# A slot per expert, three more by row number, and a folded bias in wide products (perceiver block, one core of a Trainium2 chip)

## The chip, the core and the metric

The kernel runs on one core of one Trainium2 chip. A core has a matrix engine (PE, with its own loader of stationary operands, PEld), a vector engine (DVE), an activation engine (ACT), a general engine (POOL) and a queue that only issues transfers (SP). POOL issues transfers too, those whose rows are picked by an index in memory ("indirect"). All transfers run on the core's 16 DMA engines. Each engine takes its own instructions in program order, and waits for others by semaphores. The metric is the time of one execution on the device in microseconds, as the median of several runs.

## What is computed

Two layers of a perceiver: x is 8 x 64 = 512 rows of 512 numbers, the context 8 x 1601 rows. The part that matters here is the end of layer 0 and the start of layer 1:

```python
x = x + _L0_xattn_ref(_layernorm(x), ctx_1024, ctx_1024, ...)
x = x + _L0_attn_ref(_layernorm(x), ...)          # a gated scan
x = x + _L0_ffn_ref(_layernorm(x), ...)           # eight experts, one per row
x = x + _L1_xattn_ref(ctx_1024, ctx_1024, _layernorm(x), Wk, Wv, bv, Wq, bq, Wo, bo)

def _L0_ffn_ref(x, router_w, router_b, expert_w, expert_b):
    probs = softmax(x @ router_w + router_b)
    gate, idx = max(probs), argmax(probs)
    e_out = x @ expert_w[idx] + expert_b[idx]     # expert_w: 8 x 512 x 512
    return gate * e_out

# in _L1_xattn_ref: scores = (q Wq^T + bq)(k Wk^T)^T / sqrt(512)
```

All arithmetic is in float32. An expert's weights are 1 MB. In layer 1 the kernel multiplies Wq and Wk into one matrix ahead of time ("folds" them), and then bq with Wk into one vector of 512 (`wqk_b`); Wv and Wo are folded as well.

## The kernel before

**Experts by slots.** A router gives each of the 512 rows one of eight experts. The rows are scattered to a scratch array in memory (`xsd`) so that rows of one expert lie together in blocks of 128, called slots. `SLOTS = 11` slots are enough for any routing: each expert's rows take as many slots as they need, one after the other. `places()` (L924) counts rows per expert on PE, works out on DVE where each row goes (`posi`, L950) and which expert each of the 11 slots belongs to (`wrow`, row numbers into the table of weights, L960 to L968), and has POOL scatter the rows (L953).

`slots()` (L1089) then runs over the 11 slots. `fetch(s)` (L1095) loads the 1 MB of the slot's expert into one of `WE = 4` tiles `we`, by an indirect transfer on POOL with row numbers from `wrow`. `rows(s)` (L1101) loads the slot's 128 rows (256 KB) on SP. `turn(s)` (L1105) transposes them on PE, ACT copies them out, and four products on PE (L1123) give the slot's result, which DVE copies out and SP stores to `ysd` (L1126). In turn s of the loop the order is: products of s, store of s, `fetch(s + 4)`, `rows(s + 4)`, `turn(s + 2)`. Fetches of slots 1 to 3 stand behind a POOL copy (`seen`, L1113) in the code. After the last slot POOL gathers the results back by `posi` (L1139), and x is updated (L1141).

**The work between routing and slots.** `fold_qk()` (L983) multiplies Wq and Wk: it transposes Wq into the tile `wqT`, multiplies with the tile `wk1`, and last computes `wqk_b` by 16 products whose moving operand is one column of bq (L988 to L992). `wk1` and `wqT` are tiles of the pool that held the keys of layer 0. After that pool is closed, new pools take over its memory: `wp` (weight and context tiles `w`), `md`, and `we`. `expert_bias()` (L1165) multiplies the expert biases (tile `eb`, 8 x 512) with the gates; `fold_vo()` (L1152) transposes Wv and multiplies it with Wo; the second half of that product runs after the slots.

**What sets the order.** PE's order is written out by `interleave` (L244): threads yield estimated durations, and the thread with the lowest rank that is due goes next. The order is then fixed: PE runs it as written, waiting where an operand isn't there. SP's order is the program's order too from L1576 on (`manual_schedule` of SP, until L1145). There stand, in this order: `eb` (16 KB), `cst` (448 KB), Wv and Wo (1 MB each, in halves), eight context tiles (512 KB each, for the scores of layer 1), a bias row, and then what `slots()` issues. A transfer also waits, on SP, until the eighth transfer before it has landed.

Of the kernel before, what the change touches and what calls it, by code (L numbers as in the profile page):

```python
# [16 lines left out]
NT = 4  # L17
DC = 4
SK = 1601
E, FF, CAP = 8, 2048, 64  # L20
WE = 4
SLOTS = 11
CH = [(0, 512), (512, 512), (1024, 512), (1536, 65)]
KC = [(0, 384), (384, 384), (768, 384), (1152, 449)]
SB = [(i * 128, min(128, SK - i * 128)) for i in range(13)]
# [19 lines left out]
def perceiver_kernel(ctx: ExitStack, tc: tile.TileContext, a: dict, out: bass.AP):  # L45
# [304 lines left out]
    ohs, wgt = [sm([128, NT, E], nm, 1) for nm in ("ohs", "wgt0")]  # L350
    gates = sm([128, NT], "gates", 1)
    posi = small.tile([128, NT], mybir.dt.int32, tag="posi", name="posi", bufs=1)
    wrow = small.tile([128, SLOTS], mybir.dt.int32, tag="wrow", name="wrow", bufs=1)
    xsd, ysd = [tc.dram_tile((SLOTS * 128, D), F32, name=nm) for nm in ("xsd", "ysd")]


    with ExitStack() as st:
# [20 lines left out]
        def bank(*shape):  # L378

            return ps("bk", shape or (128, 512), 7)  # L380
# [393 lines left out]
        for b in range(B):  # L774
            if b == 1:

                zero = sm([128, 64], "zero", 1)
                nc.gpsimd.memset(zero, 0.0)
                for s in range(SLOTS):
                    nc.sync.dma_start(  # L780
                        xsd[ts(s, 128), :].rearrange("p (r c) -> p r c", c=64), zero.unsqueeze(1).to_broadcast([128, 8, 64])
                    )
            if b == B - 1:

                for i in (2, 1, 0, 3):
# [12 lines left out]
                tri0, ones0, iota0 = [c3[:, ts(i, 128)] for i in range(3)]  # L798
                nc.vector.tensor_mul(c3[:, 384:], iota0, ident)
                line = sm([128, 1], "sl_line", 1)  # L800
                nc.vector.reduce_sum(line, c3[:, 384:], axis=AX.X)
                steps = sm([128, NT], "sl_steps", 1)
                nc.vector.tensor_scalar_mul(steps, iota0[:, :NT], 128.0)
                rw0 = sm([128, DC, E], "rw0", 1)
                nc.sync.dma_start(rw0, a["L0_ffn_router_w"].rearrange("(p c) e -> p c e", c=DC))
                rb0 = sm([128, E], "rb0", 1)
                nc.sync.dma_start(rb0, a["L0_ffn_router_b"].partition_broadcast(128))
            if b % 2 == 0:
                oU = xq.tile([128, DC, 128], F32, tag="oX", name=name("oU"), bufs=2)
                rq = sm([128, 16], "rq")  # L810
            if b == B - 1:
                break
            queries(b + 1)
            if b % 2:
                load_tail((b + 1) // 2)
            load_unit(b + 1, 0)
            fill = products(b + 1)

            def project(n):
                for _ in range(n):  # L820
                    next(ahead, None)
                    next(fill)

            pa = ps("pa", (128, DC, 128))


            for ec, (na, nb, nc_, nd) in enumerate(((2, 3, 2, 3), (2, 3, 2, 3), (1, 3, 2, 3), (2, 3, 3, 5))):
                att = attend(b, ec, *got.pop(ec), pa, rq)
# [24 lines left out]
            run(fill)  # L853
# [70 lines left out]
        def places():  # L924
# [7 lines left out]
            for t in range(NT):  # L932
                mm(total, ones0, ohs[:, t, :], t == 0, t == NT - 1)
            work = xq.tile([128, D], F32, tag="oX", name="work", bufs=2)
            full = work[:, : E * NT].rearrange("p (e k) -> p e k", e=E)
            nc.vector.tensor_tensor(
                full, total.unsqueeze(2).to_broadcast([128, E, NT]), steps.unsqueeze(1).to_broadcast([128, E, NT]), ALU.is_gt
            )
            used, upto = work[:, 32:40], work[:, 40:48]
            nc.vector.reduce_sum(used, full, axis=AX.X)  # L940
            nc.vector.tensor_tensor_scan(upto, ones0[:, :E], used, 0.0, ALU.mult, ALU.add)
            nc.vector.tensor_sub(used, upto, used)
            place = work[:, 64:96].rearrange("p (t e) -> p t e", e=E)
            nc.vector.scalar_tensor_tensor(
                place, used.unsqueeze(1).to_broadcast([128, NT, E]), 128.0, rank, ALU.mult, ALU.add
            )
            nc.vector.tensor_mul(place, place, ohs)
            pos = work[:, 96 : 96 + NT]
            nc.vector.reduce_sum(pos, place, axis=AX.X)
# [2 lines left out]
            for t in range(NT):  # L952
# [4 lines left out]
                    tc.declare_no_dep(i.ins, other.ins, reason="no two tokens have the same place")  # L957
                scatters.append(i)

            past = work[:, 128 : 128 + SLOTS * E].rearrange("p (s e) -> p s e", e=E)  # L960
            nc.vector.tensor_tensor(
                past, upto.unsqueeze(1).to_broadcast([128, SLOTS, E]),
                iota0[:, :SLOTS].unsqueeze(2).to_broadcast([128, SLOTS, E]), ALU.is_le,
            )
            whose = work[:, 256 : 256 + SLOTS]
            nc.vector.reduce_sum(whose, past, axis=AX.X)
            nc.vector.tensor_scalar(whose, whose, float(E - 1), 128.0, ALU.min, ALU.mult)
            nc.vector.tensor_scalar(wrow, whose, line, None, ALU.add)  # L968
# [14 lines left out]
        def fold_qk():  # L983
            yield ready[3]
            w_k, turned_ = key_tile("wk1", a["L1_xattn_Wk"]), key_tile("wqT")
            yield 5000.0
            yield from fold([w_q[:, c, :] for c in range(DC)], [w_k[:, c, :] for c in range(DC)], wqk, turned_, bank)
            p = bank()  # L988
            for e in range(DC):
                for d in range(DC):  # L990
                    mm(p[:, e : e + 1], w_k[:, d, ts(e, 128)], col("L1_xattn_bq", d), d == 0, d == 3)
            nc.vector.tensor_copy(wqk_b, p[:, :DC])  # L992

        for t in range(NT - 1):
            scan_norm(t, free[t][:, 0, :])
# [93 lines left out]
    def slots():  # L1089


        table = a["L0_ffn_expert_w"].rearrange("e (p c) d -> (e p) (c d)", c=DC)
        ws, xs, xsT = {}, {}, {}

        def fetch(s):  # L1095
            ws[s] = we.tile([128, DC * D], F32, tag="we", name=name("we"))
            nc.gpsimd.indirect_dma_start(
                ws[s], None, table, bass.IndirectOffsetOnAxis(ap=wrow[:, s : s + 1], axis=0)
            )

        def rows(s):  # L1101
            xs[s] = t2("xs")
# [6 lines left out]
        fetch(0)  # L1109
        for s in range(4):  # L1110
            rows(s)

        nc.gpsimd.tensor_copy(seen, xs[1][:, 0:1])  # L1113
        for s in range(1, WE):
            fetch(s)
        yield 13000.0
        for s in range(2):
            turn(s)
# [1 line left out]
        for s in range(SLOTS):  # L1120
            p = ps("pp")
            for c in range(DC):
                mm(p, xsT[s][:, ts(c, 128)], ws[s][:, ts(c, D)], c == 0, c == 3)  # L1123
            y = t2("ys")
            nc.vector.tensor_copy(y, p)
            nc.sync.dma_start(ysd[ts(s, 128), :], y)  # L1126
            if s + WE < SLOTS:
                fetch(s + WE)
            if s + 4 < SLOTS:
                rows(s + 4)  # L1130
            if s + 2 < SLOTS:
                turn(s + 2)
            if s == 7:

                sooner[0, 2] = context(0, 2)
            yield 0.0
# [434 lines left out]
        mh["o"], mh["wo"] = oT, wo  # L1571

    biased, asked, folded = [Event() for _ in range(3)]
    seen = md.tile([128, 1], F32, tag="seen", name="seen", bufs=1)
    in_order = ExitStack()
    in_order.enter_context(tc.manual_schedule(engines={mybir.EngineType.SP}))  # L1576
    nc.sync.dma_start(eb, a["L0_ffn_expert_b"])
    nc.sync.dma_start(cst, a["cst"])
    for n in "vo":
# [222 lines left out]
```

## Time and profile before

| What | us |
|---|---|
| median of 3 runs | 1608.79 (1601.51 to 1611.84) |
| the profiled execution, whole | 1610.92 |
| its span, first to last instruction | 1609.1 |
| PE busy in it | 1543.5 |
| from the products of `wqk_b` to the first slot's transposes | 1044.55 to 1067.71 |
| the eleven slots on PE | 1067.71 to 1119.1 |
| PE idle while the results are gathered and normalized | 5.62 and 2.14, before 1135.06 and 1138.28 |

The span is 1.8 us short of the profiled execution's time, and that execution is 2.1 us above the median. In the views, times count from the span's start. A row of the timeline gives the start, the duration, the engine (SPq and POOLq are the issuing of transfers), the source line, output and input tiles, and in brackets how long the engine had been idle before and what released it. A row of the stages gives the stretch, its length, the busy time of each engine with its instructions, the granted clock of PE as a share of full speed, the busy share of the DMA engines, and what they moved in GB/s.

### The profile page before, as it was taken

What the parts mean: (1) busy time and instruction counts of PE and PEld (TensorE: products, weight loads), DVE (VectorE), ACT (ScalarE), POOL (GpSimd) and SP (SyncE); (2) the same over time, 40 slices, a digit from 0 to 9 for tenths busy, and PEclk for the clock granted to TensorE, in tenths of its full rate; (3) what the DMA queues carried; (4) which work ended last, traced back from release to release, by engine and by line L of the source; (5) the groups of instructions that cost most, each with busy time, mean ns of one, the idle gap of its engine ahead of it and who ended that gap; (6) DMA issues with size and microseconds to landing.
All of it is one profiled execution on the core that took longest, in us unless ns stands there. A gap on an engine that the chain in (4) does not pass through costs nothing. (4 is left out here: it accounts for less than half of the span.)

```text
span 1609.1 us, 23036 instructions
## 1 busy us (share of the span) xinstructions
PE 1543.5 (96%) x9452; PEld 1123.9 (70%) x9452; DVE 719.8 (45%) x1678; ACT 291.0 (18%) x495; POOL 228.3 (14%) x274
## 2 busy tenths in 40 slices
PE   8999999999999999999999999999899898989996
PEld 6778888888888878888888868954444456654432
DVE  5245555445545455554555666521322344341213
ACT  1111212212122212122221231111001111200000
POOL 5211111111110111211021000111200121120000
PEclk9999999999999999999999999989999999979999
DMA  8100110010111111010111320478799650619995
GB/s 254 44 27 27 34 27 27 27 53 27 34 27 27 40 40 34 27 35 20 46 34 31 97 75 1 177 253 289 274 371 362 242 210 1 229 47 374 378 387 205
DMA packets 129193, 197.64 MB, mean 123 GB/s; under 512 B 27825, under 2 KB 53169, under 8 KB 127681
## 3 DMA queue, kind: packets, MB, share of 16 engines
q1 hardware_dynamic: 126864, 182.54, 33.8%
q0 software_dynamic: 2224, 13.63, 2.3%
q8 instruction: 75, 1.23, 0.3%
q14 instruction: 30, 0.24, 0.0%
HBM read 188.28 MB, written 7.86 MB: 122 GB/s over the span
## 5 line engine op out<-in xcount | busy, mean ns | idle before, releaser
L466 PE MATMUL bk<-pc,Tk 128*128 128x256 f32 x768 | 179.4, 382 | 0.2 <-POOL pc L403 0.2
L510 PE MATMUL bk<-Tv,pc 128*128 128x256 f32 x768 | 179.4, 382 | 0.0
L593 DVE TENSOR_SCALAR_CACHE_REDUCE s<-bk 128x512 f32<-128x512 f32 (+1 forms) x256 | 131.9, 572 | 101.2 <-PE bk L230 100.9
L466 PEld LDWEIGHTS bk<-pc,Tk 128*128 128x128 f32 x768 | 142.5, 190 | 29.3 <-issue 5.3
L510 PEld LDWEIGHTS bk<-Tv,pc 128*128 128x128 f32 x768 | 142.9, 190 | 23.9 <-issue 5.3
L466 PE MATMUL bk<-pc,k 128*128 128x256 f32 x576 | 136.7, 386 | 6.1 <-DMA pc<-in_ctxT_dram 6.1
L605 ACT ACTIVATE s<-s,sx_nm 128x1601 f32<-128x1601 f32 x64 | 103.9, 1626 | 193.0 <-DVE sx_nm L602 177.9
L510 PE MATMUL bk<-v,pc 128*128 128x256 f32 x576 | 134.2, 380 | 0.0
L493 DVE TENSOR_TENSOR kT<-bk,tm 128x512 f32<-128x512 f32 x96 | 66.4, 692 | 131.1 <-PE bk L466 130.4
L466 PEld LDWEIGHTS bk<-pc,k 128*128 128x128 f32 x576 | 109.5, 193 | 22.2 <-issue 7.8
L402 POOL TENSOR_TENSOR pc<-pc,pc 128x512 f32<-128x512 f32 x24 | 30.5, 1272 | 655.6 <-PE bk L510 285.4
L510 PEld LDWEIGHTS bk<-v,pc 128*128 128x128 f32 x576 | 108.1, 190 | 15.8 <-issue 1.4
L629 ACT COPY pT<-bk 128x512 f32<-128x512 f32 x96 | 56.3, 586 | 292.3 <-PE bk L235 290.9
L235 PE MATMUL bk<-ident,s 128*128 128x128 f32 (+1 forms) x832 | 103.4, 274 | 0.0
L230 PE MATMUL pa<-pT,vU 128*64 128x128 f32 x1536 | 99.3, 277 | 3.6 <-ACT pT L629 3.6
L230 PE MATMUL bk<-kT,qbd 64*128 64x512 f32 x384 | 102.7, 642 | 0.0
L235 PEld LDWEIGHTS bk<-ident,s 128*128 128x128 f32 (+1 forms) x832 | 93.1, 141 | 12.4 <-issue 5.2
L230 PEld LDWEIGHTS pa<-pT,vU 128*64 128x64 f32 x1536 | 82.4, 137 | 26.4 <-issue 18.9
L526 DVE TENSOR_TENSOR vU<-bk,tm 128x512 f32<-128x512 f32 x96 | 66.4, 692 | 72.1 <-PE bk L510 71.1
L631 DVE COPY pT<-bk 128x512 f32<-128x512 f32 (+1 forms) x128 | 75.5, 616 | 14.5 <-PE bk L235 13.9
L94 POOL TENSOR_SCALAR ln_rs<-ln_mv 128x1 f32<-128x1 f32 x32 | 10.8, 338 | 404.3 <-DVE ln_mv L1604 188.5
L230 PE MATMUL pa<-w,hT 128*64 128x512 f32 x256 | 58.6, 597 | 1.1 <-DMA w<-in_L_ffn_w_dram 1.1
(306 smaller groups left out, 1856.3 us busy)
## 6 DMA issues: line engine op xcount, KB each, us to landing
w<-in_L_ffn_w_dram SPq DMA_DIRECT2D x128, 512.0 KB, 10.7
pc<-in_ctxT_dram SPq DMA_DIRECT2D x96, 256.0 KB, 2.7
w<-in_ctxT_dram SPq DMA_DIRECT2D x48, 512.0 KB, 9.2
w<-in_ctx_dram SPq DMA_DIRECT2D x48, 512.0 KB, 8.2
pc<-in_L_xattn_Wo_dram SPq DMA_DIRECT2D x12, 256.0 KB, 2.6
w<-in_L_ffn_in_proj_w_dram SPq DMA_DIRECT2D x6, 512.0 KB, 4.8
xsd<-zero SPq DMA_DIRECT2D x11, 256.0 KB, 3.7
xs<-xsd SPq DMA_DIRECT2D x11, 256.0 KB, 8.0
```

Source lines behind the costliest of these rows:

```text
L94: nc.gpsimd.tensor_scalar_add(dst, var, 1e-5)
L230: nc.tensor.matmul(p, w, m, start=start, stop=stop)
L235: nc.tensor.transpose(p, v, ident)
L402: nc.gpsimd.tensor_add(S[0], A[1, 0], A[1, 1])
L466: nc.tensor.matmul(p[:, ts(e, 256)], Wk[i][:, d, ts(e, 128)], A[i][:, d, :], start=(d == 0), stop=(d == 1))
L493: nc.vector.tensor_add(o[:, 2 * j : 2 * j + 2, ts(i, 256)], p.rearrange("p (e s) -> p e s", e=2), s.rearrange("p (e s) -> p e s", e=2),)
L510: nc.tensor.matmul(p[:, ts(k, 256)], A[i][:, d, ts(k, 128)], Wv[i][:, d, :], start=(d == 0), stop=(d == 1))
L526: nc.vector.tensor_add(o[i][:, :, ts(j, 256)], p.rearrange("p (k e) -> p k e", k=2), s.rearrange("p (k e) -> p k e", k=2))
L593: nc.vector.tensor_scalar(s[i][:, c0 : c0 + n], p[:, :n], 1.0, None, ALU.mult, ALU.max, accum_out=mx[:, i, c0 // 512 : c0 // 512 + 1],)
L605: nc.scalar.activation(s[i], s[i], AF.Exp, bias=nm[:, i : i + 1], scale=scale, accum_out=rs[:, i : i + 1])
L629: nc.scalar.copy(o, v)
L631: nc.vector.tensor_copy(o, v)
```

## The change

1. **Slots.** Slot e (0 to 7) always belongs to expert e and takes its first 128 rows; three more slots (8 to 10) take what is left over. So the weights of slots 0 to 7 are known before routing: they are loaded by plain transfers on SP. Only slots 8 to 10 go by row number on POOL. `places()` computes a row's place in four steps on DVE in the place of one, and `wrow` shrinks from 11 to 3 columns.
2. **Order of the loads.** The weights of slots 1 to 3 are put first in SP's fixed order, ahead of `eb`, `cst`, Wv, Wo and the context. Those of slot 0 stay at the head of `slots()`, now on SP, behind the context tiles and ahead of the rows. Slots 4 to 7 are fetched in the loop on SP, between the store of slot s and the rows of s + 4. The POOL copy `seen` is gone. The third pair of context tiles is loaded one slot earlier.
3. **Folded bias.** `wqk_b` comes from 4 products with bq spread over 128 columns as stationary operand and Wk as moving operand (128 x 512), a copy by ACT into a part of the tile of Wq, 4 transposes and a copy by DVE.

```diff
-SLOTS = 11
+MORE = 3
+SLOTS = E + MORE
...
-            full = work[:, : E * NT].rearrange("p (e k) -> p e k", e=E)
+            full = work[:, : E * (NT - 1)].rearrange("p (e k) -> p e k", e=E)
...
+            nc.vector.scalar_tensor_tensor(jump, used, 128.0, firsts[:, 1, :], ALU.mult, ALU.add)
             place = work[:, 64:96].rearrange("p (t e) -> p t e", e=E)
-            nc.vector.scalar_tensor_tensor(
-                place, used.unsqueeze(1).to_broadcast([128, NT, E]), 128.0, rank, ALU.mult, ALU.add
-            )
+            nc.vector.tensor_scalar(place, rank, 128.0, None, ALU.is_ge)
+            nc.vector.tensor_mul(place, place, jump.unsqueeze(1).to_broadcast([128, NT, E]))
+            nc.vector.tensor_add(place, place, firsts[:, 0, :].unsqueeze(1).to_broadcast([128, NT, E]))
+            nc.vector.tensor_add(place, place, rank)
...
             p = bank()
+            for d in range(DC):
+                mm(p, col("L1_xattn_bq", d).to_broadcast([128, 128]), w_k[:, d, :], d == 0, d == 3)
+            nc.scalar.copy(w_q[:, 0, :], p)
+            yield COPY
+            p = bank()
             for e in range(DC):
-                for d in range(DC):
-                    mm(p[:, e : e + 1], w_k[:, d, ts(e, 128)], col("L1_xattn_bq", d), d == 0, d == 3)
-            nc.vector.tensor_copy(wqk_b, p[:, :DC])
+                flip(p[:, ts(e, 128)], w_q[:, 0, ts(e, 128)])
+            nc.vector.tensor_copy(wqk_b, chunks(p)[:, :, 0])
...
         def fetch(s):
-            ws[s] = we.tile([128, DC * D], F32, tag="we", name=name("we"))
-            nc.gpsimd.indirect_dma_start(
-                ws[s], None, table, bass.IndirectOffsetOnAxis(ap=wrow[:, s : s + 1], axis=0)
-            )
+            if s < E:
+                if s:
+                    ws[s] = we_tile()
+                nc.sync.dma_start(ws[s], table[ts(s, 128), :])
+            else:
+                ws[s] = we_tile()
+                nc.gpsimd.indirect_dma_start(
+                    ws[s], None, table, bass.IndirectOffsetOnAxis(ap=wrow[:, s - E : s - E + 1], axis=0)
+                )
...
         fetch(0)
         for s in range(4):
             rows(s)
-
-        nc.gpsimd.tensor_copy(seen, xs[1][:, 0:1])
-        for s in range(1, WE):
-            fetch(s)
...
-            if s == 7:
+            if s == 6:

                 sooner[0, 2] = context(0, 2)
...
+    first_ws = {s: we_tile() for s in range(WE)}
     in_order = ExitStack()
     in_order.enter_context(tc.manual_schedule(engines={mybir.EngineType.SP}))
+
+    for s in range(1, WE):
+        nc.sync.dma_start(first_ws[s], table[ts(s, 128), :])
     nc.sync.dma_start(eb, a["L0_ffn_expert_b"])
     nc.sync.dma_start(cst, a["cst"])
```

More of the change, by code (lines that the diff above doesn't have):

```diff
@@ L352, in perceiver_kernel @@
     posi = small.tile([128, NT], mybir.dt.int32, tag="posi", name="posi", bufs=1)
-    wrow = small.tile([128, SLOTS], mybir.dt.int32, tag="wrow", name="wrow", bufs=1)
+    wrow = small.tile([128, MORE], mybir.dt.int32, tag="wrow", name="wrow", bufs=1)
     xsd, ysd = [tc.dram_tile((SLOTS * 128, D), F32, name=nm) for nm in ("xsd", "ysd")]
@@ L803, in perceiver_kernel @@
                 nc.vector.tensor_scalar_mul(steps, iota0[:, :NT], 128.0)
+                firsts = sm([128, 2, E], "sl_firsts", 1)
+                nc.vector.tensor_scalar_mul(firsts[:, 0, :], iota0[:, :E], 128.0)
+                nc.vector.tensor_scalar(firsts[:, 1, :], iota0[:, :E], -128.0, 128.0 * (E - 1), ALU.mult, ALU.add)
                 rw0 = sm([128, DC, E], "rw0", 1)
@@ L934, in places @@
             work = xq.tile([128, D], F32, tag="oX", name="work", bufs=2)
-            full = work[:, : E * NT].rearrange("p (e k) -> p e k", e=E)
+            full = work[:, : E * (NT - 1)].rearrange("p (e k) -> p e k", e=E)
             nc.vector.tensor_tensor(
-                full, total.unsqueeze(2).to_broadcast([128, E, NT]), steps.unsqueeze(1).to_broadcast([128, E, NT]), ALU.is_gt
+                full, total.unsqueeze(2).to_broadcast([128, E, NT - 1]),
+                steps[:, 1:].unsqueeze(1).to_broadcast([128, E, NT - 1]), ALU.is_gt,
             )
-            used, upto = work[:, 32:40], work[:, 40:48]
+            used, upto, jump = work[:, 32:40], work[:, 40:48], work[:, 48:56]
             nc.vector.reduce_sum(used, full, axis=AX.X)
@@ L958, in places @@
                 scatters.append(i)
-            past = work[:, 128 : 128 + SLOTS * E].rearrange("p (s e) -> p s e", e=E)
+            past = work[:, 128 : 128 + MORE * E].rearrange("p (s e) -> p s e", e=E)
             nc.vector.tensor_tensor(
-                past, upto.unsqueeze(1).to_broadcast([128, SLOTS, E]),
-                iota0[:, :SLOTS].unsqueeze(2).to_broadcast([128, SLOTS, E]), ALU.is_le,
+                past, upto.unsqueeze(1).to_broadcast([128, MORE, E]),
+                iota0[:, :MORE].unsqueeze(2).to_broadcast([128, MORE, E]), ALU.is_le,
             )
-            whose = work[:, 256 : 256 + SLOTS]
+            whose = work[:, 256 : 256 + MORE]
             nc.vector.reduce_sum(whose, past, axis=AX.X)
@@ L1089, in slots @@
     def slots():
-        table = a["L0_ffn_expert_w"].rearrange("e (p c) d -> (e p) (c d)", c=DC)
-        ws, xs, xsT = {}, {}, {}
+        ws, xs, xsT = first_ws, {}, {}
         def fetch(s):
-            ws[s] = we.tile([128, DC * D], F32, tag="we", name=name("we"))
-            nc.gpsimd.indirect_dma_start(
-                ws[s], None, table, bass.IndirectOffsetOnAxis(ap=wrow[:, s : s + 1], axis=0)
-            )
+            if s < E:
[7 more added lines that the diff above has]
+                )
         def rows(s):
@@ L1573, in perceiver_kernel, with we_tile @@
     biased, asked, folded = [Event() for _ in range(3)]
-    seen = md.tile([128, 1], F32, tag="seen", name="seen", bufs=1)
+    table = a["L0_ffn_expert_w"].rearrange("e (p c) d -> (e p) (c d)", c=DC)
+    def we_tile():
+        return we.tile([128, DC * D], F32, tag="we", name=name("we"))
+    first_ws = {s: we_tile() for s in range(WE)}
     in_order = ExitStack()
     in_order.enter_context(tc.manual_schedule(engines={mybir.EngineType.SP}))
+    for s in range(1, WE):
+        nc.sync.dma_start(first_ws[s], table[ts(s, 128), :])
     nc.sync.dma_start(eb, a["L0_ffn_expert_b"])
```

## The prediction

> **What bounds the kernel now.** I read the page's head first, then the timelines of PE, SP and POOL around the routing, then that stretch in stages.
>
> ```profile
> span 1609.1 us, 23036 instructions
> PE 1543.5 (96%) x9452; PEld 1123.9 (70%) x9452; DVE 719.8 (45%) x1678; ACT 291.0 (18%) x495; POOL 228.3 (14%) x274
> ```
>
> PE is busy 96% of the span, so only its waits or its own instructions can move the time; the change keeps eleven slots with four products each, so PE's work on experts is what it was.
>
> PE (start, duration, line, tiles, wait before):
>
> ```profile
> 1044.55 3.63 PE L230 MATMUL bk<-cols,wk 128*128 128x1 f32 x32
> 1048.04 0.60 PE L235 MATMUL pa<-ident,wgt 128*8 128x128 f32 x4
> 1048.47 1.40 PE L235 MATMUL pp<-ident,w 128*128 128x128 f32 x8
> 1049.80 7.19 PE L230 MATMUL pa<-eb,wgtT 8*128 8x512 f32 x8
> 1056.92 1.97 PE L235 MATMUL pp<-ident,w 128*128 128x128 f32 x8
> 1058.82 9.05 PE L230 MATMUL pp<-w,wvT 128*128 128x256 f32 x32
> 1067.71 1.04 PE L235 MATMUL pt<-ident,xs 128*128 128x128 f32 x8
> ...
> 1106.03 0.63 PE L235 MATMUL pt<-ident,xs 128*128 128x128 f32 x4 [2.17 <-DMA xs<-xsd]
> 1106.49 5.29 PE L230 MATMUL pp<-we,xsT 128*128 128x512 f32 x8
> ```
>
> From the narrow products of the bias (1044.55) to the first slot (1067.71) PE has no gap, but the work is slow: eight passes over 128x512 with `eb` take 7.19 us, those of a slot take 3.60. Later a slot waits 2.17 us for its rows and then needs 5.29 us.
>
> SP and POOL (issues of transfers):
>
> ```profile
> 1024.72 0.89 SPq L1020 DMA_DIRECT2D w<-in_L_xattn_Wv_dram  x2
> ...
> 1026.68 6.64 SPq L1206 DMA_DIRECT2D w<-in_ctxT_dram  x8
> 1033.81 0.79 SPq L1041 DMA_DIRECT2D row<-in_rows_dram  x1
> 1048.37 1.77 SPq L1103 DMA_DIRECT2D xs<-xsd  x4
> ```
>
> ```profile
> 1045.68 0.96 POOL L953 DMA_INDIRECT xsd<-free,posi  x1 [0.30 <-issue]
> 1049.03 0.98 POOL L1097 DMA_INDIRECT we<-in_L_ffn_expert_w_dram,wrow  x1 [2.39 <-issue]
> ```
>
> SP had issued Wv, Wo, the context and a bias row by 1034.6, before PE needed any of it. Its next transfer, the rows, waited until 1048.37 for the scattered rows. On POOL the first indirect load of weights started at 1049.03, though `wrow` had been ready at 1041.2 and the last scatter had been issued by 1046.64: it waited 2.39 us for something else, and that ended as PE finished the bias products (1048.2). The tiles `we` take over the memory of `wk1` and `wqT`, which those products read.
>
> Stages (stretch, length, busy time PE to POOL, granted clock, DMA share, GB/s):
>
> ```profile
> 1032.00:1036.00 4.00, 4.00 (x24) 3.64 (x23) 1.95 (x11) 0.50 (x2) 0.00 (x0) 1.00 1.05 387
> ...
> 1049.00:1050.00 1.00, 1.00 (x6) 0.67 (x5) 0.95 (x2) 0.05 (x1) 0.97 (x1) 0.50 0.56 127
> 1061.00:1062.00 1.00, 1.00 (x4) 0.73 (x4) 0.00 (x0) 0.00 (x0) 0.00 (x0) 0.50 0.96 379
> 1063.00:1064.00 1.00, 1.00 (x6) 0.90 (x5) 0.06 (x1) 0.00 (x0) 0.00 (x0) 1.00 1.05 438
> ...
> 1080.00:1090.00 10.00, 8.46 (x26) 3.87 (x26) 1.39 (x2) 1.17 (x2) 1.88 (x2) 1.00 0.98 369
> 1090.00:1100.00 10.00, 8.23 (x27) 3.76 (x26) 2.08 (x3) 1.17 (x2) 2.82 (x3) 1.00 0.97 332
> ```
>
> The queue moves 387 GB/s when it is full. PE's clock is 0.50 from 1049 to 1062. The slots run at 332 to 369 GB/s with the DMA engines 97% busy: transfers, not PE, pace them.
>
> **The change part by part.**
>
> *Loads of slots 1 to 3, moved ahead on SP.* They wait for the memory as before: in the changed program as built, the first of them waits for the last wide product with `wk1` and for the copies into `wqT`. That is 1048.2, as now. But on SP everything issued up to 1034.6 now stands behind it: `eb`, `cst`, Wv, Wo, eight context tiles, the bias row, slot 0's weights, the rows. None can go before 1048.3. (`wqT`'s copies are done by 1027.1; the products decide.)
>
> Landing times: the first half of Wv (0.524 MB) landed 3.4 us after its issue, 1.35 of which are its bytes at 387 GB/s, so about 2.05 us are fixed. An issue costs SP 0.44 us for 0.5 MB, less than its bytes need, so bytes decide. From 1048.3: three weights, 3.15 MB, land at 1058.5; `eb` and `cst` (0.47 MB) at 1059.7; Wv by 1062.4; Wo by 1065.1; context, 4.19 MB, by 1076.0; bias row and slot 0's weights by 1079.4; first two slots' rows at 1080.1 and 1080.8.
>
> PE meanwhile: after the bias it transposes the gates and then needs Wv. It idles from about 1050 to 1061-1062.4. From there the row sequence of before follows: from 1048.47 to 1067.71, that is 19.2 us at the clock it had. It gives 1081.5 for the first slot's transposes; rows and weights are there by then. So the slots start 13.8 us later.
>
> *A rule of the skill.* In the row above the clock is 0.50 for 13 us while PE shows busy all the time, and rises 3.5 us after full products begin (1058.82). The Trainium skill ("TensorE: Matmul & The Clock Gate", What's actually happening) has it otherwise: one idle window of about 3.4 us halves the clock, one such window of sustained work restores it. By the page the narrow products should not have lost it, and here the idle 11 us would; PE would be fast again 3.4 us into the `eb` products, finish about 5 us earlier at 1076, and then wait for the second rows: start 1080.8. By the trace, where eight-row products did not restore the clock, it is 1081.5. I take the trace; either way the gain of a warm start is eaten by transfers.
>
> *Wide bias.* Eight passes 128x512 with a spread column are in the trace at L1161: 3.60 us (128-row timeline row at 1125.84), against 3.63 for the narrow ones. New are an ACT copy (0.59, as L874, plus about 0.2 on each side) and four transposes (0.44): +1.4 us on PE's order, hidden in PE's wait for Wv; with that cover gone it costs 1.4. It also might keep the clock up in 1049-1062, worth up to 6.7 us (19.2 minus 12.5 at full clock: 0.9 flips and 0.4, `eb` 3.4, 0.9, fold 6.9). That gain needs Wv at 1048, which the queue order takes away. I take 0.
>
> *Places and POOL.* Four more steps on DVE of 0.17 to 0.19 (L944, L947): rows scattered 0.8 us later, at about 1050; nothing reads them before 1066, when SP reaches the rows. Two steps more for `firsts` (0.2 each): beside PE's products. POOL loses eight issues of 0.94 and a copy of 0.20; it was idle next to them. All 0; without the cover, 0.8.
>
> *Slots.* Before: 51.4 us (1067.71 to 1119.1). PE's part is 11 x 3.87 = 42.6 (1072.52 to 1076.39 is one slot without a wait). The rest: waits for rows 1.00 + 0.54 + 0.22 + 1.55 + 2.17 = 5.5, the slow slot after the longest wait 1.7, and 1.6 small. After: the same bytes, 1.57 MB per slot (weights 1.05, rows and store 0.26 each). In one queue at 387 GB/s that is 4.06 us per slot. The rows of slot s + 4 are used 2 x 3.87 = 7.7 us after the end of slot s; store issue 0.9 after that end, bytes 4.06, fixed 2.05: they land after 7.0. So the first come 0.7 us in time, the backlog of 0.2 us per slot uses that up, and the last three, whose weights come by POOL and share the engines, wait a little. The DMA page ("DMA: Bandwidth & Descriptors", Queues, rings and completion order) says that an engine takes turns between queues packet by packet, and consumes one queue in ring order. That speaks against the change: rows now stand behind a full weight load rather than beside one. In the trace, rows beside a weight load took 7.6 us (1073.81 to 1081.43), against 6.1 by bytes in ring order, so ring order is no worse here. Ends: 43 (no wait at all) and 52 (no gain). I take 46: gain 5.4.
>
> *After the slots* the gather and normalization follow the last store as before, with 10.6 us of Wv Wo products beside them: shifted, not changed.
>
> Sum: +13.8 - 5.4 = +8.4. On the profiled execution's 1610.9 that is 1619.3; the median of the runs shown is 2.1 lower: 1617.2, rounded 1617, 0.5% slower.
>
> **The rivals.**
>
> *A. Slots gain nothing and PE cools in them.* Rows land late: at the 332 GB/s of the stage 1090-1100, 1.57 MB take 4.73 us, 0.86 above PE's 3.87; from a slack of 0.7, seven slots lose 5.3, and each wait of about 2 us brings the 1.7 of a half clock, say twice: 42.6 + 1.6 + 5.3 + 3.4 = 52.9. With 13.8 and the 1.4 of the bias, +16.7: 1625.5. It decides from rows landing 7.7 us after the end of the slot that issued them. For: the slow slot at 1106.49. Against: 387 GB/s of plain loads.
>
> *B. Loads go early, as the words of the change say.* If the memory of slots 1 to 3 were free at 1024.7, when Wv's was: 11.2 MB up to slot 0's weights are in by 1055.7, Wv by 1039; PE has no wait, the clock may hold (up to -6.7, plus 1.4 for the bias), slots -5.4: -10.7, 1598. Against: POOL's wait up to 1049.03 in the trace, and the wait of the moved load. It would show as first loads of `we` near 1025.
>
> *C. Slots at PE's pace, start set by rows:* 1080.8 - 1067.7 + 42.6 - 51.4 = +4.3: 1613. For: 387 GB/s in plain queues.
>
> **How the numbers follow.** Forecast with C as its lower part: 0.66. A and worse: 0.28. B: 0.04; anything else faster or slower 0.02. A measurement of this kernel tells about 1% from no change: 16 us. Forecast and C lie within it (0.67), A beyond (0.29; its bound 1624.9 lies just under A's 1625.5), B mostly under -1% or near (0.04). The range for 8 in 10 runs from C with the spread of the runs before (1601.5 to 1611.8, 5 us to a side), 1610, to A with as much above, 1630.
>
> **What would show it.** Right: the first plain loads of `we` at about 1048.3; SP silent before it from 957 on; Wv at 1055 to 1060 issued, PE idle some 11 us before its transposes; clock 0.50 from about 1052; first slot near 1081; slots in 44 to 48. Wrong: loads of `we` or Wv near 1025; no gap on PE after the bias; `eb` products at 3.4 us; slots over 51.

## The result, and the profile after

The changed kernel takes 1621.53 us (median of 7 runs, 1618.72 to 1626.18), the kernel before 1606.51 in the same set (7 runs, 1601.51 to 1611.84): ratio 1.0107, 95% interval 1.0088 to 1.0127. It is 15.0 us slower. The profiled execution of the changed kernel took 1621.53 us as well; the profiled one of before, at 1610.92, lay 4.4 above its median, which will matter.

The head of the page of the changed kernel:

```profile
span 1619.6 us, 23002 instructions
PE 1540.4 (95%) x9432; PEld 1120.3 (69%) x9432; DVE 721.5 (45%) x1684; ACT 291.3 (18%) x496; POOL 220.2 (14%) x265
```

PE is busy 3.1 us less than before over a span that is 10.5 us longer: the time went into PE's waits, not into its work. The timeline of SP shows what came late (start, duration, line, transfer, count):

```profile
954.01 0.51 SPq L1630 DMA_DIRECT2D rw<-in_L_ffn_wg_dram  x1
1050.06 1.29 SPq L1596 DMA_DIRECT2D we<-in_L_ffn_expert_w_dram  x3
...
1052.58 0.94 SPq L1032 DMA_DIRECT2D w<-in_L_xattn_Wv_dram  x2
1053.56 1.75 SPq L1032 DMA_DIRECT2D w<-in_L_xattn_Wo_dram  x2
1057.40 9.83 SPq L1218 DMA_DIRECT2D w<-in_ctxT_dram  x8
...
1070.74 4.34 SPq L1119 DMA_DIRECT2D xs<-xsd  x4
```

SP issues nothing between 954.5 and 1050.06. Wv, which went out at 1024.72 before, goes out at 1052.58; the first rows, 1048.37 before, at 1070.74. The view of SP's waits names what held the first of the moved loads (line, what it waited for: total, times, longest):

```profile
SPq L1596 <- DVE wqT L335: 74.1, 1, 74.1
SPq L1596 <- PE bk L231: 21.4, 1, 21.4
```

First the copies into `wqT`, then the products on PE that read `wk1`, the last of which are the wide bias products. On PE's timeline the delay looks like this (the bracket gives the idle time ahead of the row and what ended it):

```profile
1046.40 3.60 PE L231 MATMUL bk<-wk,cols 128*128 128x512 f32 x8
1050.67 0.66 PE L236 MATMUL bk<-ident,wq 128*128 128x128 f32 x4 [0.68 <-ACT wq L999]
1051.16 0.60 PE L236 MATMUL pa<-ident,wgt 128*8 128x128 f32 x4
1062.59 0.69 PE L236 MATMUL pp<-ident,w 128*128 128x128 f32 x2 [10.83 <-DMA w<-in_L_xattn_Wv_dram]
1063.95 1.54 PE L236 MATMUL pp<-ident,w 128*128 128x128 f32 x6 [0.67 <-DMA w<-in_L_xattn_Wv_dram]
1065.42 7.19 PE L231 MATMUL pa<-eb,wgtT 8*128 8x512 f32 x8
1072.54 1.97 PE L236 MATMUL pp<-ident,w 128*128 128x128 f32 x8
1074.44 9.00 PE L231 MATMUL pp<-w,wvT 128*128 128x256 f32 x32
1083.27 1.04 PE L236 MATMUL pt<-ident,xs 128*128 128x128 f32 x8
...
1101.82 0.63 PE L236 MATMUL pt<-ident,xs 128*128 128x128 f32 x4 [1.90 <-DMA xs<-xsd]
...
1120.57 0.63 PE L236 MATMUL pt<-ident,xs 128*128 128x128 f32 x4 [3.03 <-DMA xs<-xsd]
```

It shows one gap of 10.83 us ended by Wv, then the same row sequence as before at the same half clock (`eb` products 7.19 us in both), and two waits for rows in the slots. The stages (stretch, length, busy time PE, PEld, DVE, ACT, POOL; granted clock, DMA share, GB/s):

```profile
1020.00:1050.00 30.00, 29.99 (x187) 26.03 (x185) 14.96 (x49) 4.14 (x10) 5.05 (x7) 1.00 0.09 33
1050.00:1055.00 5.00, 1.09 (x8) 0.73 (x8) 0.84 (x2) 0.59 (x1) 0.00 (x0) 0.93 0.82 290
1055.00:1078.00 23.00, 14.74 (x32) 8.26 (x33) 4.13 (x6) 1.17 (x2) 0.00 (x0) 0.50 1.04 396
```

From 1020 to 1050 the DMA engines moved 33 GB/s, where before they moved 380 to 387 from 1032 to 1044. What was not moved then is moved at 396 GB/s while PE waits for it.

### The profile page after: what moved, and what is told of

Same layout as the page of the kernel before. It is cut to its first block, busy times and chain, and to the rows that moved or that the text cites. A ratio compares the mean times of both kernels' runs of the same rounds, so it can differ in the third digit from the quotient of the medians.

```text
span 1619.6 us, 23002 instructions
## 1 busy us (share of the span) xinstructions
PE 1540.4 (95%) x9432; PEld 1120.3 (69%) x9432; DVE 721.5 (45%) x1684; ACT 291.3 (18%) x496; POOL 220.2 (14%) x265
## 5 line engine op out<-in xcount | busy, mean ns | idle before, releaser
L632 DVE COPY pT<-bk 128x512 f32<-128x512 f32 (+1 forms) x128 | 75.5, 616 | 14.6 <-PE bk L236 13.9
```

The lines of the kernel that those rows point to most:

```text
L632: nc.vector.tensor_copy(o, v)
```

## The experiments

Each run was timed in turn with the kernel before on the same chip; ratios are to those runs (1604.6 to 1605.5 us). "To the slots" is the time from the start of the products of `wqk_b` to the first slot's transposes, "slots" from there to the second half of the fold behind them, each from the one profiled execution. That execution can lie off its median: by 6.7 us for the loads behind Wo (1621.73 us), by 3.4 for the wide bias alone, by 2.9 for one load ahead, by 2.5 for two ahead. So a few us between two "slots" figures need not show in the medians.

| Kernel | to the slots | slots | median us | ratio, 95% interval |
|---|---|---|---|---|
| before, first profile | 23.16 | 51.22 | 1606.51 | |
| before, again | 23.15 | 47.63 | 1605.15 | 1.0000 (0.9989 to 1.0011) |
| changed | 36.87 | 48.51 | 1621.53 | 1.0107 (1.0088 to 1.0127) |
| changed, narrow bias | 36.95 | 47.21 | 1620.08 | 1.0097 (1.0079 to 1.0116) |
| changed, one load ahead | 30.87 | 50.99 | 1617.22 | 1.0073 (1.0054 to 1.0092) |
| changed, loads behind Wo | 28.63 | 54.91 | 1615.03 | 1.0070 (1.0055 to 1.0086) |
| changed, other memory, three ahead | 29.43 | 47.28 | 1612.33 | 1.0050 (1.0034 to 1.0067) |
| changed, other memory, two ahead | 19.95 | 48.50 | 1605.70 | 0.9998 (0.9987 to 1.0009) |
| changed, loads behind the rows | 19.95 | 48.38 | 1605.08 | 1.0003 (0.9992 to 1.0013) |
| changed, loads on POOL | 19.96 | 46.55 | 1604.52 | 0.9997 (0.9983 to 1.0010) |
| before, wide bias | 19.95 | 52.08 | 1604.87 | 0.9999 (0.9989 to 1.0010) |
| loads on POOL, 128-row bias | 18.44 | 47.77 | 1603.24 | 0.9988 (0.9979 to 0.9997) |
| the same, rows first | 18.43 | 49.83 | 1604.49 | 0.9999 (0.9986 to 1.0013) |
| before, wide and 128-row bias | 18.44 | 49.10 | 1602.51 | 0.9987 (0.9975 to 1.0000) |

### Is it the place of the three loads in SP's order?

The three loads go behind the first rows, all else stays changed:

```diff
-    for s in range(1, WE):
-        nc.sync.dma_start(first_ws[s], table[ts(s, 128), :])
...
         for s in range(4):
             rows(s)
+        for s in range(1, WE):
+            nc.sync.dma_start(ws[s], table[ts(s, 128), :])
```

> The changed kernel with one thing undone: the loads of slots 1 to 3 stand behind the first rows again, the rest of the change stays. Queue theory (they hold up all of SP until the bias products are done): SP issues Wv, Wo and the context near 1025 again, PE's gap of 10.8 us before the transposes of Wv is gone, the first slot starts some 13.7 us earlier than in the changed kernel; 1621.5 - 13.7 = 1608, or down to 1601 if the wide products also keep PE's clock up. Rival (plain weight loads ahead of the rows in one ring, in the slot loop, cost the time): the slots stay as slow and the kernel stays above 1618.

1605.08 us, ratio 1.0003: with this one edit the whole loss is gone. On PE the gap between the bias and the fold is gone with it:

```profile
1045.15 3.60 PE L231 MATMUL bk<-wk,cols 128*128 128x512 f32 x8
1049.42 0.66 PE L236 MATMUL bk<-ident,wq 128*128 128x128 f32 x4 [0.68 <-ACT wq L999]
...
1051.32 3.88 PE L231 MATMUL pa<-eb,wgtT 8*128 8x512 f32 x8
...
1056.59 8.68 PE L231 MATMUL pp<-w,wvT 128*128 128x256 f32 x32 [0.36 <-DVE wvT L335]
1065.10 1.04 PE L236 MATMUL pt<-ident,xs 128*128 128x128 f32 x8
```

The `eb` products now take 3.88 us in place of 7.19: PE did not go cold between the bias and them. The slots, the places, the wide bias and the plain loads of slots 4 to 7 are as in the changed kernel, so together they cost and bring nothing that shows.

In the next run the same loads went to POOL's queue, at the head of `slots()`, so that SP is free of them and their wait:

```diff
-        fetch(0)
+        for s in range(WE):
+            nc.gpsimd.dma_start(ws[s], table[ts(s, 128), :])
         for s in range(4):
             rows(s)
...
-    for s in range(1, WE):
-        nc.sync.dma_start(first_ws[s], table[ts(s, 128), :])
```

> The changed kernel with the loads of slots 0 to 3 as plain transfers on POOL, which waits there for the same memory while SP goes on. Queue theory: the wait is the same (first load near the end of the bias), and costs nothing, since nothing that PE needs stands behind it on POOL: first slot as in the kernel before or earlier, 1601 to 1606. Rival (the loads themselves, not their place, are what delays PE): near 1620.

1604.52 us, ratio 0.9997, again the time of before. On POOL's timeline the loads come here:

```profile
1050.22 2.18 POOL L1126 DMA_DIRECT2D we<-in_L_ffn_expert_w_dram  x4 [1.62 <-ACT wq L999]
```

POOL had to wait too, and its loads begin 0.16 us later than SP's in the changed kernel. So the same three megabytes, with slot 0's, go out at the same moment from another queue, and cost nothing: nothing that PE needed soon was queued behind them.

### The wait at the head, or the bytes ahead?

Four runs grade the two parts of the delay. In the first, the three loads stand behind Wv and Wo but ahead of the context and the rows.

```diff
-    for s in range(1, WE):
-        nc.sync.dma_start(first_ws[s], table[ts(s, 128), :])
...
     for n in "vo":
         wn[n] = weights(a["L1_xattn_W" + n])
+    for s in range(1, WE):
+        nc.sync.dma_start(first_ws[s], table[ts(s, 128), :])
     for c in range(2):
         sooner[0, c] = context(0, c)
```

> The changed kernel with the loads of slots 1 to 3 behind Wv and Wo, still ahead of the context. Queue theory, in two parts: Wv is early, so PE has no gap before its transposes; but the context, slot 0's weights and the rows are behind 3.1 MB and start only at the end of the bias, so the first rows land after 2.05 us and 8.9 MB at 387 GB/s, 25 us after the bias in place of 19: PE waits some 6 us for rows, and the time lies 6 us above that of the version with the loads behind the rows, about 1610 to 1614. Rival (only Wv's lateness counts): no wait for rows, same time as that version.

1615.03 us, ratio 1.0070, a little above the range expected. PE runs through to the end of the fold, and the wait turns up one place later (SP's timeline, then PE's):

```profile
1050.11 1.29 SPq L1600 DMA_DIRECT2D we<-in_L_ffn_expert_w_dram  x3
1051.44 9.49 SPq L1218 DMA_DIRECT2D w<-in_ctxT_dram  x8
...
1064.07 4.34 SPq L1119 DMA_DIRECT2D xs<-xsd  x4
```

```profile
1057.87 8.41 PE L231 MATMUL pp<-w,wvT 128*128 128x256 f32 x32
1075.07 1.97 PE L236 MATMUL pt<-ident,xs 128*128 128x128 f32 x8 [8.79 <-DMA xs<-xsd]
1076.92 5.65 PE L231 MATMUL pp<-we,xsT 128*128 128x512 f32 x8
```

SP is held until the same moment, but the first to suffer are the rows, issued at 1064.07 behind the context: PE idles 8.79 us, and then the first slot runs at a low clock (5.65 for 3.60).

In the second, only slot 1, the load that waits for `wk1` and `wqT`, is ahead; slots 2 and 3 stand behind the rows:

```diff
-    for s in range(1, WE):
-        nc.sync.dma_start(first_ws[s], table[ts(s, 128), :])
+    nc.sync.dma_start(first_ws[1], table[ts(1, 128), :])
...
         for s in range(4):
             rows(s)
+        for s in range(2, WE):
+            nc.sync.dma_start(ws[s], table[ts(s, 128), :])
```

> The changed kernel with only slot 1 loaded ahead (it is the one that waits for wk1 and wqT); slots 2 and 3 come behind the first rows. Theory (SP is held until 1050 by the wait, and what stands ahead of Wv adds its transfer time): the hold stays, two megabytes fewer stand ahead of Wv, 2 MB / 390 GB/s = 5.4 us: the first slot 8 to 9 us late instead of 13.7, 1613 to 1617 us. If only the bytes counted: a third of the loss, about 1610. If only the hold counted: 1621.

1617.22 us, just above the 1613 to 1617 expected. The gap ahead of Wv is 5.81 us in place of 10.83, 5.0 less for two megabytes fewer (5.4 expected from 390 GB/s), and the first slot 6.0 us earlier than in the changed kernel. So of the 13.7 us that the changed kernel loses up to the slots, 6.0 were two of the three megabytes, and 7.7 remain with one load and the hold.

The third shortens the wait without moving anything in the order: the pool of the weights goes to the other end of memory.

```diff
-    we = routed.enter_context(tc.tile_pool(name="we", bufs=WE, reuse_waits="tile"))
+    we = routed.enter_context(tc.tile_pool(name="we", bufs=WE, reuse_waits="tile", side="right"))
```

> The changed kernel with the same order on SP, all three loads ahead, but the tiles of the expert weights at the other end of memory. The third tile then waits for the copy of posi at 1043.5 us instead of the bias products at 1050. Theory (the time is set by when the last of the three waits ends): SP goes on 6.5 us earlier and two of the three megabytes have gone out before: Wv issued at about 1045 and landed by 1051, PE without a gap or with one under 3 us before eb and the fold, then a wait of 2 to 5 us for the rows behind Wo and the context: 1606 to 1611 us. Rival (moving the loads ahead costs by their place in the queue, not by the wait): 1619 to 1624 us as for the changed kernel.

1612.33 us, over half of the loss gone, though the time is a little above the 1606 to 1611 expected. The waits of the three loads are now these (SP's waits):

```profile
SPq L1596 <- DVE posi L958: 48.9, 1, 48.9
SPq L1596 <- PE bk L236: 28.0, 1, 28.0
...
SPq L1596 <- DVE s L594: 5.6, 1, 5.6
SPq L1596 <- PE pa L231: 5.5, 1, 5.5
```

The third load waits longest, for the copy of `posi`, and SP goes on at 1042.2. I had expected Wv to land 6 us after its issue; it was issued at 1043.12 and ended PE's wait at 1052.92, after 9.8, beside the third load and POOL's scatters (DMA at 202 and 286 GB/s in the two 3 us stretches from 1042 to 1048). That left a gap of 3.09 us, and with it the half clock for `eb` (7.19 us). Still, the same loads in the same place in the queue cost 9 us less. This run alone does not say whether by the earlier end of the wait or by the two megabytes that were out before it: the run with one load ahead also has one megabyte behind the hold; there the hold ends 8.0 us later (1050.25), and yet the first slot came only 1.4 us later behind the bias (30.87 for 29.43).

The fourth separates them. With the same memory and only slots 1 and 2 ahead, no load waits for anything late:

```diff
-    for s in range(1, WE):
+    for s in range(1, 3):
         nc.sync.dma_start(first_ws[s], table[ts(s, 128), :])
...
         for s in range(4):
             rows(s)
+        nc.sync.dma_start(ws[3], table[ts(3, 128), :])
```

> The changed kernel with the tiles of the expert weights at the other end of memory, where the last readers of the tiles for slots 1 and 2 are a softmax and a weighting at 962 and about 990 us; only slots 1 and 2 are loaded ahead, slot 3 comes behind the first rows. Theory (what cost the time was the wait on wk1 and wqT at the head of SP's queue, not loading ahead as such): SP is free, Wv goes out at 1024 to 1026 as before, PE has no gap between the bias and the first slot (that stretch 20 us, as with the loads moved back), and two megabytes fewer have to be moved beside the slots: 1599 to 1604 us, as fast as the kernel before or a little faster. Rival (two megabytes ahead of Wv and Wo delay them whatever the place in memory): a gap on PE after the bias, 1610 us or more.

1605.70 us, ratio 0.9998, just above the 1599 to 1604 expected. SP's timeline:

```profile
988.27 6.30 SPq L1597 DMA_DIRECT2D we<-in_L_ffn_expert_w_dram  x2
...
1026.42 0.89 SPq L1032 DMA_DIRECT2D w<-in_L_xattn_Wv_dram  x2
```

Two experts' weights go out from 988.27 on, Wv at 1026.42 (1024.72 before), and the loss is gone, though two megabytes stand ahead of Wv in the queue. So the place ahead costs nothing by itself; a wait that ends late at that place does. But nothing is gained either: the slots still took 48.5 us.

### What is the wide bias worth?

In the changed kernel with the narrow products put back (the diff of the change, reversed for this part):

> The changed kernel with the narrow bias products (32 of one column) back in place of the wide ones. They end 0 to 1 us from where the wide ones end, so the loads go out at the same time, and PE has a gap of 11 us behind them either way. Theory (the form of the bias is hidden by the gap): within 2 us of the changed kernel, 1620 to 1624 us. Rival (the wide form keeps the clock up and is worth 3 us here as well): 1624 to 1626 us.

1620.08 us; its interval overlaps that of the changed kernel. The bias is hidden there by the gap, which is 12.27 us with the narrow products. Alone on the kernel before, it is not hidden:

```diff
-            for e in range(DC):
-                for d in range(DC):
-                    mm(p[:, e : e + 1], w_k[:, d, ts(e, 128)], col("L1_xattn_bq", d), d == 0, d == 3)
-            nc.vector.tensor_copy(wqk_b, p[:, :DC])
+            for d in range(DC):
+                mm(p, col("L1_xattn_bq", d).to_broadcast([128, 128]), w_k[:, d, :], d == 0, d == 3)
+            nc.scalar.copy(w_q[:, 0, :], p)
...
```

> The kernel before with the wide bias products alone. Clock theory N (the one-column products lose PE's clock): the clock stays at 1.00 through the products with eb, which take 3.5 us in place of 7.2; from the bias to the first slot 17 us in place of 23.2, 1606.5 - 5.3 = 1601. Clock theory E (the eight-row products with eb do not hold the clock, whatever stands before): the clock falls to 0.50 a few us later, at most 3 us are gained, and the copy and the four transposes on PE's order take 1.4 back: 1604 to 1608.

1604.87 us, ratio 0.9999. In the trace the first slot comes 19.95 us behind the bias in place of 23.15, since the clock stays at 1.00 through the `eb` products. In this profile the 3.2 us went again in the slots (one wait for rows of 5.41 us); the execution took 1608.25 us, the longest of its fourteen. Some of the gain is lost inside the stage itself: behind the `eb` products the clock falls after all. To see whether those do it, `eb` and `wgtT` were filled up to 128 rows with zeros, on top of the run with the loads on POOL:

```diff
-    eb = act.tile([E, D], F32, tag="sq", name="eb", bufs=2)
-    wgtT = act.tile([E, D], F32, tag="sq", name="wgtT", bufs=2)
+    eb = act.tile([128, D], F32, tag="sq", name="eb", bufs=2)
+    wgtT = act.tile([128, D], F32, tag="sq", name="wgtT", bufs=2)
+    for z in (eb, wgtT):
+        nc.gpsimd.memset(z, 0.0)
...
-    nc.sync.dma_start(eb, a["L0_ffn_expert_b"])
+    nc.sync.dma_start(eb[:E, :], a["L0_ffn_expert_b"])
...
-            nc.vector.tensor_copy(wgtT, p[:E, :])
+            nc.vector.tensor_copy(wgtT[:E, :], p[:E, :])
```

> The kernel with the loads of slots 0 to 3 as plain transfers on POOL, and eb and wgtT filled up with zero rows to 128, so that the products of the expert bias have 128 rows instead of eight; the result is the same. Theory (eight-row products let the clock fall, as it does for 3.5 us behind them in the traces with the wide bias): the granted clock stays 1.00 from the bias to the slots, the fold takes 7.1 us instead of 8.7, the first slot comes 18.3 us behind the bias instead of 20.0; in the total 1602 to 1605 us, since rows bound the slots. Rival (something else lets the clock fall): the fold takes 8.7 us as before.

1603.24 us, ratio 0.9988 (0.9979 to 0.9997). The stages of the run without this edit, and then of the run with it:

```profile
1055.00:1057.00 2.00, 2.00 (x11) 1.07 (x10) 1.61 (x3) 0.00 (x0) 0.00 (x0) 1.00 1.00 415
1057.00:1060.00 3.00, 2.64 (x7) 2.13 (x7) 0.37 (x1) 0.58 (x1) 0.00 (x0) 0.52 1.05 434
```

```profile
1055.00:1057.00 2.00, 2.00 (x10) 1.05 (x9) 1.47 (x3) 0.00 (x0) 0.00 (x0) 1.00 1.02 423
1057.00:1060.00 3.00, 2.49 (x14) 2.02 (x13) 0.91 (x3) 0.58 (x1) 0.00 (x0) 1.00 1.02 423
```

The third number from the end of a row is the granted clock: 0.52 from 1057 to 1060 becomes 1.00. The products themselves take as long (3.88 and 3.86 us), but the fold behind them takes 7.17 us in place of 8.69. The transposes between them are the same, and PE's gap ahead of the fold is even longer (0.51 us for 0.36), so neither of these is what let the clock fall. The same two edits on the kernel before, without any of the moved loads:

> The kernel before with the wide bias products and with the expert bias in products of 128 rows (eb and wgtT filled up with zero rows; the result is the same); no load of weights is moved and every slot's weights come by the indirect transfer. Theory (what the run with the loads on POOL gained, 2 us, came from the clock, not from the loads): the clock is 1.00 from the bias to the slots, the first slot 18.4 us behind the bias, 1602 to 1604 us. Rival (the clock's gain is taken back by the waits for rows unless the loads are plain and ahead): 1604.5 to 1606 us, with longer waits for rows in the trace.

1602.51 us, ratio 0.9987 (0.9975 to 1.0000): as good, so the moved loads are not needed for it. What little there is to gain here comes with the clock. It is the lowest median of all the runs; its interval reaches to no change, and the next run, at the same clock, shows no gain.

### Do rows wait behind weights in the queue?

The last edit has, in the loop, the rows of slot s + 4 loaded ahead of its weights:

```diff
-            if s + WE < SLOTS:
-                fetch(s + WE)
             if s + 4 < SLOTS:
                 rows(s + 4)
+            if s + WE < SLOTS:
+                fetch(s + WE)
```

> The same, and in the loop of the slots the rows of slot s+4 are loaded ahead of the weights of slot s+4 instead of behind them. Theory (rows of 256 KB land after 8 us since they stand behind a megabyte of weights in the same queue): the rows land after 4 to 6 us, the waits for rows inside the slots go, 1599 to 1602 us. Rival (the waits for rows come from the load of the transfer engines as a whole): the weights land later instead, and the time is that of the run without this part within 1.5 us.

1604.49 us, 1.25 more than without the edit; the slots took 49.83 us, with waits of 1.02 and 3.59 for rows. The expected gain did not come. The waits ahead of slots 4 to 7, whose weights come by SP, sum to 1.02 us and to 1.99 without the edit, in one profile each. But the 3.59 is for slot 8. Its weights come by POOL, so the edit leaves its rows where they were in SP's queue, behind the weights issued at 1081.93: issued at 1085.32, they were used at 1096.69, 11.4 us later, and from 1088 on POOL's loads took 48 to 67% of the transfer engines' time. That points to the load of the engines, but no run measures it by itself.

### How good was the first profile of before?

> The kernel before, unchanged, for a second profile of it. The first one was of an execution that took 1610.9 us, 4.4 above its median. Theory (its slots waited for rows longer than they mostly do): the bias starts within 2 us of 1044.6, the first slot 23.2 us behind it as in the first profile, and the slots take 45 to 48 us rather than 51.4, so that there was little for the slots of the changed kernel to gain. Rival (the excess of the first profile lay elsewhere): the slots again take 50 to 52 us. The ratio to itself says what a ratio of this size is worth: 0.998 to 1.002.

Ratio 1.0000 with an interval of 0.0011 to either side. Rows of PE's timeline in this second profile of the kernel before:

```profile
1046.09 3.63 PE L230 MATMUL bk<-cols,wk 128*128 128x1 f32 x32
...
1069.24 1.04 PE L235 MATMUL pt<-ident,xs 128*128 128x128 f32 x8
...
1101.80 0.63 PE L235 MATMUL pt<-ident,xs 128*128 128x128 f32 x4 [1.52 <-DMA xs<-xsd]
1102.26 3.60 PE L230 MATMUL pp<-we,xsT 128*128 128x512 f32 x8
1105.70 0.60 PE L235 MATMUL pt<-ident,xs 128*128 128x128 f32 x4
1106.13 3.60 PE L230 MATMUL pp<-we,xsT 128*128 128x512 f32 x8
...
1116.87 7.07 PE L230 MATMUL pp<-w,wvT 128*128 128x256 f32 x32
```

To the first slot it takes 23.15 us as in the first profile (23.16). But the slots take 47.63 us and not 51.22. The longest wait of the first profile, 2.17 us for the rows of slot 9 with products of 5.29 behind it, is not there: slot 9's transposes (1105.70) follow at once, and the products behind them take 3.60. The wait of 1.52 is for slot 8, where the first profile had 1.55. Over the twelve runs the slots took from 46.55 to 54.91 us; the way to them took 19.95 or 19.96 in all four runs with the same work on PE and no wait.

## Why the prediction was right on the cause and too low on the time

Against the second profile of before (span 1604.0, near its median), the span of 1619.6 divides as follows: 0.3 before the bias, 13.72 from the bias to the first slot, 0.88 in the slots, and 0.7 after them, 15.6 in all.

- **Loads waiting on `wk1`, and SP behind them: right.** The forecast was +13.8 to the first slot, measured 13.72. It holds step by step, so the agreement is not luck: the loads went out at 1050.06, 3.66 us after the bias began (3.75 forecast) and 0.06 behind its products; Wv's second half had landed 13.9 us after that (14.1 forecast); from there to the first slot it took 19.3 (19.2 forecast). Undoing the move took all of it back, and 3.2 us more up to the slots (36.87 became 19.95), since the wide bias is then no longer covered.
- **PE's gap and the clock behind it: right.** An idle stretch of 10.83 us; the clock at 0.50 from 1055 to 1078, through the `eb` products. The prediction had set the row of the trace above the Trainium skill ("TensorE: Matmul & The Clock Gate", What's actually happening), by which about 3.4 us of sustained work bring the clock back; here 7.19 us of eight-row products did not.
- **Wide bias 0: right in this order.** Uncovered, it brought 3.2 us up to the slots and nothing at the end. The bound of 6.7, or 5.3 with the 1.4 that the wide form was put at, would have needed the 128-row `eb` too; with both, 23.15 became 18.44, a gain of 4.7.
- **Places and POOL 0: no sign against it.** With the loads put back they are all still in, at a ratio of 1.0003 (0.9999 with the wide bias alone).
- **Slots, -5.4: this is the term that failed.** The changed kernel's slots took 48.51 us, not the 46 forecast, and the 51.4 from which it was taken was one execution's: against the second profile's 47.63 there was 1.6 to gain even at 46. The step inside it that was mis-sized is the landing of the rows, put at 6.1 us behind their issue by bytes in one queue at 387 GB/s. The rows that ended the two waits of 1.90 and 3.03 us were issued here and let PE go on at 1101.82 and 1120.57, 8.0 and 9.6 us later:

```profile
1093.83 0.40 SPq L1119 DMA_DIRECT2D xs<-xsd  x1
...
1110.99 0.36 SPq L1119 DMA_DIRECT2D xs<-xsd  x1
```

Other rows were early enough: those issued at 1089.91 were in use 6.0 us later. At the first wait only SP's queue was moving, but at 284 GB/s and not at 387 (the stage row below). At the second, POOL was loading by row number. The two rows below it, of the DMA view from 1114 to 1121, give packets, MB and share of the engines' time for POOL's queue and then for SP's, in which the rows stood:

```profile
1095.00:1100.00 5.00, 4.92 (x15) 2.10 (x13) 0.73 (x2) 0.59 (x1) 0.00 (x0) 1.00 0.86 284
...
q0 software_dynamic: 246, 1.86, 72.7%
q1 hardware_dynamic: 249, 0.46, 17.3%
```

The prediction had this sharing in words, "wait a little", and no number for it.

- **The base.** 1617 was the sum for a median of 1608.8; the median of seven runs was 1606.5. The base was thus 2.3 too high, and 1617 lay nearer to 1621.5 than the sum deserved: that is luck. In the sum, +8.4 was forecast and +15.0 measured; 6.3 of the 6.6 between are the slots.
- **Rivals.** A had the time nearly right (+16.7) and half of the reason: the slots gained nothing, but they did not cool, the clock was 1.00 from 1083 to 1130. B, loads that go early, did not happen, and where it was made to happen in part, with two loads at 988, it gave 1605.7 and not 1598. C needed slots at PE's pace and did not occur.

Not settled: what makes the rows land late in one execution and not in another, and so where the 3.2 us of the wide bias go. That POOL's loads hold up the rows is read from the trace; no run takes the weights of slots 8 to 10 off POOL. Why the engines moved only 284 GB/s at the first wait is not known, and a context load moved out of the slots was not tried.

## What to carry to other kernels

A transfer that is moved to the head of a fixed queue takes its wait with it. Ask first when the memory it writes becomes free, and what stands behind it in the queue: here three loads, the first of which was used 38 us after it went out (slot 1's products at 1088.58), held back Wv, which was needed at once. A load that has to wait goes last, or on a queue with nothing urgent behind it, or into memory that is free early. And before a gain is summed up from waits for transfers, take a second profile of the kernel before: the waits in one execution may not be the usual ones.

## What the hardware showed that was not expected

- Products of eight rows over 128x512 let the clock fall though PE is 100% busy with them: in the run with the loads on POOL they began at 1052.16 at clock 1.00, PE was busy without a break up to 1057, and the clock was 0.52 from 1057 to 1060. The 32 products of one column did the same: the kernel before fell to 0.50 at 1049, 4.5 us after their start, and with the wide form it did not. With `eb` and `wgtT` filled up to 128 rows, most of them zero, the clock stayed at 1.00.
- After a fall, full products brought the clock back within 3.2 to 4.2 us (before: products from 1058.82, clock 0.50 until 1062 and 1.00 from 1063).
- Time gained ahead of a stage that waits for transfers was worth next to nothing: 3.2 us less in four runs gave ratios from 0.9997 to 1.0003, 4.7 us less in three gave 0.9987, 0.9988 and 0.9999. Time lost there by late transfers was not free: 13.7 us up to the slots, 15.0 at the end.
